# Time attention in half-key tiles: scores for the queries that see the keys, exchanged halves in the second tile, and layer-norm roots kept in PSUM

## The chip, the cores and the metric

The kernel runs on one core of a Trainium2 chip. The core has five engines with their own instruction streams: TensorE (PE, matrix products; PEld is its weight load), VectorE (DVE), ScalarE (ACT), GpSimd (POOL) and SyncE (SP, which issues transfers). Two memories matter: SBUF, the working memory with 128 partitions, and PSUM, eight banks of 512 fp32 elements a partition, into which TensorE writes. The metric is the device time of one execution in microseconds (us), the median of several runs. A profiled execution has its own time and a span, from its first to its last instruction.

## The reference: what is computed

One layer works on x of shape (2, 256, 128, 128): batch, time, band, channel, all fp32. Everything is 65,536 tokens of 128 channels.

```
xt = layernorm(x) by token, over time: for each band
x  = x + attention(xt, 4 heads of 32, key time <= query time)
xf = layernorm(x), over bands: for each time
x  = x + attention(xf, 4 heads of 32, |key band - query band| <= 16)
x  = x + W2 gelu(W1 layernorm(x) + b1) + b2
```

The change touches the first of the three, the attention over 256 times with its causal mask. A layer norm's root is 1/sqrt(variance + 1e-5) for each token.

## The kernel before

**Groups.** Work goes in groups of 512 tokens, four tiles of 128. There are 128 groups of time attention (`OverTime`), each with two bands (`s` = 0, 1) of 256 times, so that each band has a first tile of 128 keys and a second one. After them come 128 groups of attention over bands (`OverBands`) and 128 of the feed-forward (`FeedForward`), interleaved in runs of eight.

**Order.** `BoundedPath.run` (line 1046 on) is one loop over n, written out by hand: an iteration holds steps of several groups (n - 2 to n + 12), and each engine executes its instructions in exactly the order in which they stand there (`InOrder`, whose `pinned` is line 870: that is why every line of the profile reads L870, and why the tiles' names tell the operations apart). In the time stage an iteration n has, engine by engine:

- TensorE: the scores of two groups mixed (`time_scores`: second tiles of group n, first tiles of n + 1), then the row sums `rp` and the weighted values `op` of group n - 1 (`weigh`), the output product `yp` of n - 2, and the query, key and value products `qp`, `kp`, `vp` of n + 2.
- ScalarE: exponentials of heads 0 and 3 of the second tiles, of heads 1 and 2 of the first tiles, of heads 1 and 2 of the second tiles; `ln` and `r` (one over the row sums, by Ln and Exp) of n - 1; exponentials of heads 0 and 3 of the first tiles; then `qT` and `kT` out of PSUM, the root of group n + 5 (`root_by_scalar`: `lnv` by Ln, `root` by Exp with scale -1/2), and `v` out of PSUM.
- VectorE: statistics of group n + 5 (`stats`, `mv`), `normalize` (`xh`) and `turn` (`z`) of n + 4, the residual `res` of n - 2 (`finish`), three operations of `divide` for n - 1 (the last, `oT`, reads `op`), and the root of n + 5 made exact by one Newton step (`refine`: `vy`, `vy`, `rstd`, operations on 128x4 elements).
- GpSimd: the causal mask of the second tiles (`mask_second`), a sum of exponentials (`add`), the mask of the first tiles (`mask_first`), the other `add`, and the residual with its bias row (`bias`: `res<-x,orow`).
- SyncE: four transfers that write `turned` out of `z`, the fetch of `xnT`, the loads of x and the stores of the result.

**Scores.** For a head h, whose 32 channels lie on 32 partitions, `first_scores` multiplies 128 keys of the first tile with all 256 queries of the band, and `second_scores` 128 keys of the second tile with the 128 queries of the second tile. Each uses a 32-row strip of TensorE, so four heads can run side by side; their outputs lie in eight banks, one per head and tile. An fp32 product is two records of matmul in the trace.

**Banks.** The eight banks have roles that rotate from iteration to iteration. Banks a1 and a2 (first tiles of heads 1 and 2) always stay; they also take `yp` and `qp`. `rp` and `op` go to b0 and b3, which are the next iteration's a0 and b1:

```
b = self.banks
Attention.place = dict(rp=b["b0"], op=b["b3"], yp=b["a1"], qp=b["a2"], kp=b["b1"], vp=b["b2"])
...
self.banks = dict(
    a1=b["a1"], a2=b["a2"], b0=b["a0"], b3=b["a3"], a0=b["b0"], a3=b["b1"], b1=b["b3"], b2=b["b2"]
)
```

So the second-tile scores of head 1 overwrite the bank whose `op` was last read by `oT`, and wait for it.

Of the kernel before, what the change touches and what calls it, by code (L numbers as in the profile page):

```python
# [10 lines left out]
F32 = mybir.dt.float32  # L11
# [3 lines left out]
ALU = mybir.AluOpType  # L15
# [4 lines left out]
P = 128  # L20
H = 4
# [4 lines left out]
NT = 4  # L26
# [6 lines left out]
HALF = P // 2  # L33
# [47 lines left out]
def shifted_path(tc, k, x, out):  # L81
# [5 lines left out]
    with ExitStack() as ctx:  # L87
# [36 lines left out]
        def norm_transposed(src, w_col, b_col):  # L124
# [18 lines left out]
            return xnT  # L143

        def attention(src, dst, which, banks, mask, exp_after):


# [280 lines left out]
class Group:  # L428
# [30 lines left out]
        gpsimd.tensor_scalar(self.rstd, self.mv[:, :, 1], EPS, None, ALU.add)  # L459
        gpsimd.tensor_tensor(self.rstd, self.rstd, path.k.mhalf, ALU.pow)  # L460

    def root_by_scalar(self):

        path = self.path
        ln = path.small.tile([P, NT], F32, name="lnv")
        path.scalar.activation(ln, self.mv[:, :, 1], AF.Ln, bias=path.eps)
        self.root0 = path.small.tile([P, NT], F32, name="root0")
        path.scalar.activation(self.root0, ln, AF.Exp, scale=-0.5)

    def refine(self):  # L470

        path, vector, y = self.path, self.path.vector, self.root0
        t = path.small.tile([P, NT], F32, name="vy")
        vector.scalar_tensor_tensor(t, self.mv[:, :, 1], EPS, y, ALU.add, ALU.mult)
        vector.scalar_tensor_tensor(t, t, -0.5, y, ALU.mult, ALU.mult)
        self.rstd = path.small.tile([P, NT], F32, name="rstd", bufs=16)
        vector.scalar_tensor_tensor(self.rstd, t, 1.5, y, ALU.add, ALU.mult)
# [62 lines left out]
    def values(self):  # L540
        pass
# [19 lines left out]

class Attention(Group):
    which = None
    place = {}

    def bias(self):
# [23 lines left out]
    def values(self):  # L590
        path = self.path
        wv = path.k.wf[self.which][:, 2 * P : 3 * P]
        self.vp = path.bank([P, NT, P], "vp", self.place.get("vp"))
        for i in range(NT):
            product(path, self.vp[:, i], self.xnT[:, i * P : (i + 1) * P], wv)

    def take_values(self):
        path = self.path
# [43 lines left out]
def rows_of(h):  # L642
    return slice(h * D, (h + 1) * D)


def product(path, out, weights, x, start=True, stop=True):


    for c in range(P // D):
        path.tensor.matmul(out[rows_of(c)], weights[:, rows_of(c)], x, start=start, stop=stop)  # L650


class OverTime(Attention):

    which = 0
    early, late = (1, 2), (0, 3)

    def first_tiles(self):  # L660
# [10 lines left out]

    def first_scores(self, h, s):
        r, a = rows_of(h), 2 * s * P
        self.path.tensor.matmul(
            self.s0[h][:, s], self.kT[r, a : a + P], self.qT[r, a : a + 2 * P], start=True, stop=True
        )

    def second_scores(self, h, s):
        r, a = rows_of(h), (2 * s + 1) * P
        self.path.tensor.matmul(  # L680
            self.s1[h][:, s], self.kT[r, a : a + P], self.qT[r, a : a + P], start=True, stop=True
        )

    def first_weights(self, heads):
        for h in heads:
# [3 lines left out]
        for h in heads:  # L689
            self.path.scalar.activation(self.p1[:, :, h, 0], self.s1[h], AF.Exp)  # L690

    def mask(self, blk):
        path = self.path
        path.gpsimd.affine_select(
            out=blk, in_=blk, compare_op=ALU.is_ge, fill=path.zero, base=0,
            pattern=[[0, 2], [0, H], [1, P]], channel_multiplier=-1,
        )

    def mask_first(self):
        self.mask(self.p0[:, :, :, 0:P])  # L700

    def mask_second(self):
        self.mask(self.p1[:, :, :, 0])

    def add(self, s):
        self.path.gpsimd.tensor_tensor(self.p1[:, s, :, 1], self.p1[:, s, :, 0], self.p0[:, s, :, P : 2 * P], ALU.add)
# [168 lines left out]
class BoundedPath:  # L875
# [170 lines left out]
    def run(self, x, out):  # L1046
        groups = list(self.groups(x, out))

        def do(n, *names):
            if 0 <= n < len(groups):  # L1050
                for name in names:
                    getattr(groups[n], name)()

        def at(n, kind):
            return 0 <= n < len(groups) and isinstance(groups[n], kind)

        def do_at(n, kind, *names):
            if at(n, kind):
                do(n, *names)


        run0 = [i for i in range(len(groups)) if at(i, OverBands)][: RUN // NT]
        due = dict(zip(run0, (-5, -4, -4, -3, -1, 0, 1, 2)))
        due = {n: [i for i in run0 if run0[0] + due[i] == n] for n in range(-12, len(groups) + 2)}
        A = RUN // NT

        self.scalar.preload_act_table_set(EXP_SET)
        for n in range(-12, len(groups) + 2):
            feeds = [at(n - 2 + i, FeedForward) for i in range(5)]
            bands = [at(n - 2 + i, OverBands) for i in range(5)]  # L1070
            turn = feeds[2] and bands[1]
            old, new = (groups[i] if at(i, OverTime) else None for i in (n, n + 1))
            if bands[2] and feeds[1]:
                self.scalar.preload_act_table_set(EXP_SET)
            do_at(n + 4, FeedForward, "root")
            do(n, "first_half", "first_function", "first_mask")
            if old is not None or new is not None:
                time_scores(old, new)
                b = self.banks
                Attention.place = dict(rp=b["b0"], op=b["b3"], yp=b["a1"], qp=b["a2"], kp=b["b1"], vp=b["b2"])  # L1080
            else:
                Attention.place = {}
            if old is not None:
                old.second_weights(old.late)
            if new is not None:
                new.first_weights(new.early)
            if old is not None:
                old.second_weights(old.early)
                old.mask_second()
                old.add(0)  # L1090
            if turn:
                do(n, "second_half", "second_function")
            do_at(n + 3, OverTime, "fetch")
            do_at(n + 2, (OverBands, FeedForward), "fetch")

            for i in (2 * n + 12, 2 * n + 13) if n < -2 else (n + 10,) if n < 2 else ():
                if i >= NT:
                    do(i, "load")
            if n < -8 or n >= 0:
                do(n + 12, "load")  # L1100
            if n >= 0:
                do_at(n + 5, OverTime, "statistics")
                for i in due[n]:
                    do(i, "statistics")
            do_at(n + 3, (OverBands, FeedForward), "normalize", "turn")
            do_at(n + 4, OverTime, "normalize", "turn")
            if n < 0:
                do(n + 5, "statistics")
            do_at(n + 5, FeedForward, "statistics")
            if n == -4:  # L1110
                self.fold_rest()
                self.warm()
            do(n - 1, "weigh")
            do(n - 1, "invert_exactly" if turn else "invert")
            if new is not None:
                new.first_weights(new.late)
                new.mask_first()
            if old is not None:
                old.add(1)
            if bands[2] or turn or old is not None:  # L1120
                do(n - 2, "output", "finish")
            do(n - 1, "divide")
            if not turn:
                do(n, "second_half", "second_function")
            if n in run0:
                do(n, "bias")
            if not bands[2] and old is None:
                do_at(n, FeedForward, "bias")
                do_at(n + A, OverBands, "bias")
                if at(n - 1, FeedForward) and at(n - 2, OverBands):  # L1130
                    do_at(n + A - 1, OverBands, "statistics", "root")
                if not turn:
                    do_at(n + A, OverBands, "statistics", "root")
            do_at(n + 2, OverTime, "queries_keys", "take_query", "take_key")
            do_at(n + 1, OverBands, "queries_keys", "take_query", "take_key")
            do_at(n + 5, OverTime, "root_by_scalar", "refine")
            for i in due[n]:
                do(i, "root_by_scalar", "refine")
            do_at(n, OverTime, "bias")
            if not bands[2] and not turn and old is None:  # L1140
                do(n - 2, "output", "finish")
            do_at(n + 2, OverTime, "values", "take_values")
            do_at(n + 1, OverBands, "values", "take_values")
            if old is not None or new is not None:
# [5 lines that stand above are left out]
# [69 lines left out]
```

## Time and profile before

| what | us |
|---|---|
| median of 3 runs | 2706.51 (2705.36 to 2706.72) |
| profiled execution: its time | 2703.05 |
| profiled execution: its span | 2701.3 |
| TensorE busy | 2662.7 |
| VectorE busy | 2280.2 |
| ScalarE busy | 1848.3 |
| GpSimd busy | 1868.7 |
| time stage, from one group's scores to the next | 7.311 (mean over groups 8 to 124) |

The time stage takes the first 950 us or so of the span; its first scores start at 30.7 us and its last ones near 950. A line of groups reads: line, engine, operation, output<-inputs, shapes, count, then busy us in total and mean ns of one, then idle time before them. A line of the timeline reads: start in us, length in us, engine, line, operation, output<-inputs, shape, and how many in a row are merged. TensorE's ends are modelled, and busy TensorE is not TensorE at its peak; starts are the better guide.

### The profile page before, as it was taken

The page shows a single profiled execution, that of the slowest core. Times are in us where ns is not written, and L with a number is a line of the kernel's source. Part 1 is how long each engine was busy: PE and PEld are TensorE (multiplying, and loading weights), DVE is VectorE, ACT ScalarE, POOL GpSimd, SP SyncE. Part 2 cuts the span into 40 slices and gives each one's busy share as a digit, 9 for nine tenths or more (in the row PEclk, how much of TensorE's full clock was granted, in tenths as well). Part 3 has the DMA queues.
Part 4 walks back from the last instruction along what each step waited for, and adds up shares of the span by engine and source line. Part 5 has one row for each costly group of instructions (what it writes and reads, how often), then busy time and mean ns, then how long its engine had stood idle before and what let it go on. Part 6 is the DMA issues. An engine that isn't in the chain of part 4 may idle for free.

```text
span 2701.3 us, 148062 instructions
## 1 busy us (share of the span) xinstructions
PE 2662.7 (99%) x64566; PEld 1824.9 (68%) x64566; DVE 2280.2 (84%) x6708; ACT 1848.3 (68%) x3620; POOL 1868.7 (69%) x2169
## 2 busy tenths in 40 slices
PE   7999999999999999999999999999999999999998
PEld 5667666767676666666666666666666766666665
DVE  7999999999999997868769779688697796886874
ACT  6888888888888874655746646557456465565573
POOL 3888788878888886667657666666676666665762
PEclk9999999999999999999999999999999999999999
DMA  5555555555555535445444444454444444544433
GB/s 151 142 151 143 145 151 144 149 146 142 151 144 148 150 101 129 111 121 132 109 127 124 115 125 116 121 128 116 120 124 117 121 119 121 135 108 121 129 100 82
DMA packets 471477, 346.55 MB, mean 128 GB/s; under 512 B 43296, under 2 KB 405152, under 8 KB 470816
## 3 DMA queue, kind: packets, MB, share of 16 engines
q1 hardware_dynamic: 469568, 335.92, 47.8%
q8 instruction: 508, 8.32, 1.3%
q14 instruction: 153, 1.25, 0.2%
q10 hardware_dynamic: 1248, 1.05, 0.2%
HBM read 169.03 MB, written 167.77 MB: 125 GB/s over the span
## 4 chain that ended last, share of the span: by engine, by line
PE 83%; DVE 13%; DMA 2%; issue 1%; ACT 0%; SPq 0%; DVEq 0%; ACTq 0%
PE bank L870 83%; DVE xh L870 3%; DVE bank L870 3%; DVE stats L870 2%; DVE z L870 2%; DVE u L870 2%; DMA xnT<-turned 1%; DVE x L870 1%; DVE mv L870 1%; DMA turned<-z 0%; SPq L870 0%; DMA x<-in_x 0%; DVE oT L870 0%; DMA rows_sb<-in_rows 0%; ACT p L870 0%
## 5 line engine op out<-in xcount | busy, mean ns | idle before, releaser
L870 ACT ACTIVATE hT<-bank,b 128x512 f32<-128x512 f32 x512 | 347.1, 688 | 536.0 <-PE bank L870 517.0
L870 POOL TENSOR_SCALAR_AFFINE_SELECT pf<-pf 128x512 f32<-128x512 f32 x768 | 478.5, 638 | 246.8 <-ACT pf L870 220.5
L870 DVE TENSOR_SCALAR xh<-x,mv,rstd 128x160 f32<-128x160 f32 x1536 | 597.1, 431 | 14.2
L870 PEld LDWEIGHTS bank<-w2T_sb,hT 128*32 128x32 f32 x16384 | 459.7, 110 | 63.1 <-issue 38.8
L870 PE MATMUL bank<-xnT,wf 128*32 128x512 f32 x4096 | 488.6, 592 | 2.0 <-ACT p L870 2.0
L870 PE MATMUL bank<-w2T_sb,hT 128*32 128x128 f32 x16384 | 477.5, 273 | 0.5 <-ACT hT L870 0.2
L870 PE MATMUL bank<-xnT,w1f 128*32 128x512 f32 x4096 | 474.2, 592 | 0.0
L870 ACT ACTIVATE p<-bank 128x512 f32<-128x512 f32 (+1 forms) x1024 | 417.3, 499 | 15.1 <-PE bank L870 3.8
L870 POOL TENSOR_SCALAR_AFFINE_SELECT p<-p 128x1024 f32<-128x1024 f32 x256 | 280.9, 1097 | 188.2 <-ACT p L870 188.2
L870 DVE TENSOR_TENSOR res<-bank,res 128x512 f32<-128x512 f32 x256 | 171.1, 668 | 229.1 <-PE bank L870 227.2
L870 PE MATMUL bank<-qT,kT 32*64 32x80 f32 (+2 forms) x12288 | 346.9, 275 | 4.2 <-DVE oT L870 2.2
L870 PEld LDWEIGHTS bank<-wf,xnT 128*32 128x32 f32 x8192 | 235.5, 110 | 154.4 <-issue 135.9
L870 PEld LDWEIGHTS bank<-qT,kT 32*64 32x64 f32 (+1 forms) x12288 | 298.0, 148 | 58.7 <-ACT kT L870 48.2
L870 POOL TENSOR_TENSOR p<-p,p 128x512 f32<-128x512 f32 x256 | 329.2, 1286 | 10.7
L870 DVE BATCH_NORM_STATS2 stats<-x 128x6 f32<-128x128 f32 x1536 | 326.9, 275 | 0.9 <-DMA x<-in_x 0.9
L870 ACT ACTIVATE pf<-bank 128x512 f32<-128x512 f32 x512 | 267.1, 602 | 50.9 <-PE bank L870 48.8
L870 DVE STREAM_TRANSPOSE z<-xh 128x512 f32<-128x512 f32 x384 | 273.3, 712 | 13.4
L870 PEld LDWEIGHTS bank<-xnT,w1f 128*32 128x32 f32 x4096 | 156.4, 110 | 189.4 <-issue 159.3
L870 POOL TENSOR_SCALAR rstd<-mv 128x4 f32<-128x4 f32 x248 | 56.7, 229 | 312.8 <-DVE mv L870 311.3
L870 PE MATMUL bank<-wf,xnT 128*32 128x128 f32 x8192 | 272.6, 273 | 0.0
L870 PE MATMUL bank<-wn,oT 128*32 128x128 f32 x8192 | 271.7, 273 | 0.0
L870 POOL TENSOR_TENSOR rstd<-rstd,mhalf 128x4 f32<-128x4 f32 x248 | 257.0, 1036 | 20.7
(93 smaller groups left out, 3770.3 us busy)
## 6 DMA issues: line engine op xcount, KB each, us to landing
turned<-z SPq DMA_DIRECT2D x1536, 64.0 KB, 2.2
xnT<-turned SPq DMA_DIRECT2D x384, 256.0 KB, 3.1
x<-in_x SPq DMA_DIRECT2D x128, 256.0 KB, 4.1
x<-res SPq DMA_DIRECT2D x256, 128.0 KB, 2.4
x<-x SPq DMA_DIRECT2D x128, 256.0 KB, 4.2
out<-res SPq DMA_DIRECT2D x256, 128.0 KB, 2.5
w1T_sb<-in_w1T ACTq DMA_DIRECT2D x1, 256.0 KB, 6.5
w2T_sb<-in_w2T ACTq DMA_DIRECT2D x1, 256.0 KB, 7.9
```

Of the source, the lines that this page charges most:

```text
L870: return self.tc.keep_in_program_order(emit(*args, **kwargs))
```

## The change

Four things change in the time attention, and nothing in the other two parts.

1. A first-tile score product is cut into two, of 64 keys each: keys 0 to 63 with all 256 queries, keys 64 to 127 with the 192 queries from 64 on, which are those that can see them. Positions that are left out keep what the bank held, and the mask sets them to zero after the exponential.
2. A second-tile score product is cut likewise: keys 64 to 127 with the queries 64 to 127, keys 0 to 63 with all 128. Their halves are exchanged: keys 64 to 127 go to partitions 0 to 63, keys 0 to 63 to partitions 64 to 127. So that the weights meet the right values, the value products of the second tiles (1 and 3) put their rows in the same exchanged order (`turn=2`). The mask of the second tile becomes two selects, one for each half of the partitions.
3. The root by ScalarE is written to bank a2 in PSUM, four columns of it, in the place where the first-tile exponentials of head 2 have just been read from. It is made right after the exponentials of heads 1 and 2 of the first tiles, in the iteration after the one where it stood.
4. The exact root (`refine`) moves from the end of the iteration, behind `divide`, to just ahead of `normalize` of the same group.

The instructions that each engine executes in a steady iteration are otherwise the same and in the same order.

```diff
-    def root_by_scalar(self):
+    def root_by_scalar(self, to=None):
...
-        self.root0 = path.small.tile([P, NT], F32, name="root0")
+        self.root0 = path.small.tile([P, NT], F32, name="root0") if to is None else to
         path.scalar.activation(self.root0, ln, AF.Exp, scale=-0.5)
+
+    def root_in_bank(self):
+        path = self.path
+        self.root_by_scalar(path.ps[path.banks["a2"]][:, 0:NT])
...
-            product(path, self.vp[:, i], self.xnT[:, i * P : (i + 1) * P], wv)
+            product(path, self.vp[:, i], self.xnT[:, i * P : (i + 1) * P], wv, turn=2 if i in self.swapped else 0)
...
-        path.tensor.matmul(out[rows_of(c)], weights[:, rows_of(c)], x, start=start, stop=stop)
+        path.tensor.matmul(out[rows_of(c)], weights[:, rows_of((c + turn) % NT)], x, start=start, stop=stop)
...
     which = 0
+    swapped = (1, 3)
...
     def first_scores(self, h, s):
         r, a = rows_of(h), 2 * s * P
-        self.path.tensor.matmul(
-            self.s0[h][:, s], self.kT[r, a : a + P], self.qT[r, a : a + 2 * P], start=True, stop=True
-        )
+        for e in range(0, P, HALF):
+            self.path.tensor.matmul(
+                self.s0[h][e : e + HALF, s, e:], self.kT[r, a + e : a + e + HALF], self.qT[r, a + e : a + 2 * P],
+                start=True, stop=True,
+            )
 
     def second_scores(self, h, s):
         r, a = rows_of(h), (2 * s + 1) * P
-        self.path.tensor.matmul(
-            self.s1[h][:, s], self.kT[r, a : a + P], self.qT[r, a : a + P], start=True, stop=True
-        )
+        for e in range(0, P, HALF):
+            q = P - HALF - e
+            self.path.tensor.matmul(
+                self.s1[h][e : e + HALF, s, q:], self.kT[r, a + q : a + q + HALF], self.qT[r, a + q : a + P],
+                start=True, stop=True,
+            )
...
     def mask_second(self):
-        self.mask(self.p1[:, :, :, 0])
+        self.mask(self.p1[0:HALF, :, :, 0], -HALF)
+        self.mask(self.p1[HALF:P, :, :, 0, 0:HALF])
...
             if new is not None:
                 new.first_weights(new.early)
+            do_at(n + 4, OverTime, "root_in_bank")
             if old is not None:
                 old.second_weights(old.early)
...
-            do_at(n + 4, OverTime, "normalize", "turn")
+            do_at(n + 4, OverTime, "refine", "normalize", "turn")
...
-            do_at(n + 5, OverTime, "root_by_scalar", "refine")
```

More of the change, by code (lines that the diff above doesn't have):

```diff
@@ L563 @@
     which = None
+    swapped = ()
     place = {}
@@ L643, in rows_of, with product @@
     return slice(h * D, (h + 1) * D)
-def product(path, out, weights, x, start=True, stop=True):
+def product(path, out, weights, x, start=True, stop=True, turn=0):
     for c in range(P // D):
-        path.tensor.matmul(out[rows_of(c)], weights[:, rows_of(c)], x, start=start, stop=stop)
+        path.tensor.matmul(out[rows_of(c)], weights[:, rows_of((c + turn) % NT)], x, start=start, stop=stop)
 class OverTime(Attention):
     which = 0
+    swapped = (1, 3)
     early, late = (1, 2), (0, 3)
@@ L690, in second_weights, with mask @@
             self.path.scalar.activation(self.p1[:, :, h, 0], self.s1[h], AF.Exp)
-    def mask(self, blk):
+    def mask(self, blk, base=0):
         path = self.path
         path.gpsimd.affine_select(
-            out=blk, in_=blk, compare_op=ALU.is_ge, fill=path.zero, base=0,
-            pattern=[[0, 2], [0, H], [1, P]], channel_multiplier=-1,
+            out=blk, in_=blk, compare_op=ALU.is_ge, fill=path.zero, base=base,
+            pattern=[[0, 2], [0, H], [1, blk.shape[-1]]], channel_multiplier=-1,
         )
```

## The prediction

> **What bounds the kernel now.** I read the page first: the span, the busy line and the 40 slices. TensorE is busy in every slice; VectorE is at 90% or more in the first thirteen full slices, which are the time attention that the change edits, and falls off after them.
>
> ```profile
> span 2701.3 us, 148062 instructions
> ...
> PE 2662.7 (99%) x64566; PEld 1824.9 (68%) x64566; DVE 2280.2 (84%) x6708; ACT 1848.3 (68%) x3620; POOL 1868.7 (69%) x2169
> ...
> DVE  7999999999999997868769779688697796886874
> ```
>
> "PE 99%" does not tell which of the two sets the pace, so I went to the timeline of one group (start, length, engine, operation), then to the groups by form of the whole stage.
>
> ```profile
> 502.28 0.30 ACT L870 ACTIVATE lnv<-mv,eps 128x4 f32<-128x4 f32 x1
> ...
> 502.53 1.63 PE L870 MATMUL bank<-qT,kT 32*128 32x128 f32 x32
> 502.61 0.20 ACT L870 ACTIVATE root<-lnv 128x4 f32<-128x4 f32 x1
> ...
> 503.08 1.26 POOL L870 TENSOR_TENSOR res<-x,orow 128x512 f32<-128x512 f32 x1
> ...
> 503.31 1.05 DVE L870 SCALAR_TENSOR_TENSOR vy<-mv,root 128x4 f32<-128x4 f32 x1
> 503.38 2.19 ACT L870 ACTIVATE p<-bank 128x256 f32<-128x256 f32 x6
> ...
> 504.09 1.07 PE L870 MATMUL bank<-p,ones 128*32 128x256 f32 x16
> 504.40 0.17 DVE L870 SCALAR_TENSOR_TENSOR vy<-vy,root 128x4 f32<-128x4 f32 x1
> 504.60 0.16 DVE L870 SCALAR_TENSOR_TENSOR rstd<-vy,root 128x4 f32<-128x4 f32 x1
> 504.68 0.86 DVE L870 BATCH_NORM_STATS2 stats<-x 128x6 f32<-128x128 f32 x4
> ...
> 505.74 1.58 DVE L870 TENSOR_SCALAR xh<-x,mv,rstd 128x160 f32<-128x160 f32 x4
> ...
> 509.86 1.62 PE L870 MATMUL bank<-qT,kT 32*128 32x128 f32 x32
> ...
> 510.02 0.69 DVE L870 TENSOR_TENSOR oT<-bank,u 128x512 f32<-128x512 f32 x1
> ```
>
> ```profile
> L870 DVE SCALAR_TENSOR_TENSOR vy<-mv,root 128x4 f32<-128x4 f32 x114 | 120.1, 1053 | 0.0
> ...
> L870 DVE SCALAR_TENSOR_TENSOR vy<-vy,root 128x4 f32<-128x4 f32 x114 | 18.6, 163 | 3.9
> ```
>
> Call the first weight load of a score step S (502.53). The next is at 509.86; over groups 8 to 124 the mean period is 7.311 us, and about 124 periods make the stage. VectorE's starts follow each other without a hole over 100 ns all the way round: it is the bound. Its strangest entry is vy, 1053 ns for four elements, where the same operation a line later takes 163: vy ends at 504.37, just after POOL's res (503.08 + 1.26 = 504.34). TensorE is nearly level: its weight load for the last four second-tile scores (heads 1 and 2) starts at 503.448, 52 ns after oT ends (503.396), because head 1's bank is the one whose op oT still reads. That wait cost about 0.05 us.
>
> **What the Trainium skill says.** "SBUF — State Buffer", section "Who interferes with whom": a VectorE instruction with two SBUF inputs contends with a GpSimd instruction that reads SBUF, one with a single SBUF input does not. The trace agrees: vy (both in SBUF) stretches to 1053 ns, while u and oT (one input in PSUM) stay at 692 beside running POOL work. "TensorEngine Tiling (Array Packing)", section "Key Properties": tiles run independently and changing the mode drains the array; the trace shows four streams side by side in the score step and about 0.09 us between stages of different tiling. "TensorE: Matmul & The Clock Gate", section "Architectural detail: the array is 16× 32×32, not 1× 128×128": VectorE and ScalarE are strict first-in first-out. So a VectorE wait holds all that stands behind it, which decides below.
>
> **Part by part, per group.**
>
> *Scores.* One row strip (a head) streams 2 x (256 + 128) = 768 columns today. At 213 ns a record of 256 columns and two records a matmul that is 1.28 us; with the first load (0.107), the 0.05 wait and the 0.09 drain it makes the 1.56 from 502.53 to 504.09. Afterwards each half strip streams 2 x (256 + 64) or 2 x (192 + 128), 640 either way: 1.07 us, with a load of 0.053. Left alone the step would be 1.07 + 0.05 + 0.09 and some skew, about 1.27. The records double to 64; the band scores already run such a step in 1.00 us (1422.32 to 1423.32), their last 24 records at 21 ns each, so issue stays below streaming. TensorE alone would need 7.31 - 0.29 = 7.02. Exchanging the halves and turning two value products adds no instruction. Exponentials keep their sizes; where no query sees a key they run over what the bank held, and the mask clears it.
>
> *Second mask.* One select of 1024 elements a partition (1.10) becomes one of 1024 and one of 512, each on 64 partitions. The nearest rows give 1.10 and 0.64; if half the partitions cost half, 0.55 and 0.32; if the smaller cost like the larger, 2.19. I take 1.74 less overlap, +0.58 on POOL, hidden in its 1.30 idle before the select.
>
> *Refinement.* vy reads the root from PSUM: 1053 becomes about 165 (0.15 to 0.25; no row shows this form). VectorE's work drops to about 6.5.
>
> *Order.* The two root activations no longer stand before the v copy; they follow the first-tile exponentials of heads 1 and 2, and the three refinements now stand after the statistics and **ahead of xh**. So xh, z, res, three divisions and oT wait for a root made in the same group; in the old order the root was half a microsecond old when wanted. The transpose's four DMA issues and the fetch on SP come with it, about 0.3 later in the group; xnT is used over a period after landing, no cost. The projection of queries waits for the refinement's end (S + 3.4) and starts near S + 4.6: no cost.
>
> **The new chain, from S.** Head 0's second scores end 0.05 earlier (smaller load), so the first exponential starts at 0.80 instead of 0.85. The starts of the next operations follow by 0.281, 0.264, 0.478 and 0.477 (measured starts of the exponentials), Ln to Exp 0.331, Exp 0.206: the root is there at 2.84. Handing over 0.035, three refinements 3 x 0.197 = 0.591: xh at 3.46. From xh's start to oT's end today: 510.714 - 505.744 = 4.97, unchanged. oT ends at 8.43. The last scores of the *next* group wait for it: 0.052 handover, 0.053 load, four records of 128 columns 0.436, drain 0.09, together 0.63: the row sums start at 9.06. From row sums to the following S: 509.86 - 504.091 = 5.77. That is S two groups later: 14.83, a period of **7.415**. The other floors are lower: TensorE 7.02, VectorE 6.5, ACT about 6.4, and POOL's chain (second select at 3.5, its five operations end at 8.9, then row sums' second half to S, 5.53: 14.4 over two groups, 7.22). So VectorE idles about 0.75 us a group, oT ends 1.02 after the next S where TensorE would like it by 0.75, and the score step measures about 1.65 instead of 1.56: both savings are there and the wait eats them. 124 x (7.415 - 7.311) = +12.9 us; fill and drain of the stage I take as nothing (a few one-off steps, +-2). Against the profiled 2703.05 (span 2701.3) that gives 2716; the median of the runs is 3.5 higher, so 2706.5 + 13 = 2719.5.
>
> **Rivals.** (1) *The freed VectorE is enough*: if the two-group chain is 0.22 us shorter than I sum, the period falls to 7.31, and below that it gains. The chain has four hand-overs that I read off other places. For it: VectorE loses 0.89 of work and TensorE 0.29. Against: even a root 0.2 earlier only breaks even. With POOL's chain next the period is 7.22, -11 us, 2695; with both loose 7.02, 2670. This ends on the other side; its place is xh's wait for the root, its price 0.75 us of VectorE idling. (2) *Even*: the chain within 0.1 of 14.62. (3) *POOL takes over*: selects at 2.19 make its chain 14.9, period 7.45, 2724; with TensorE also waiting for the sums, up to 7.55, 2736. For it: POOL has 0.3 us of slack before the row sums' second half. (4) *The edit doesn't do what it says*: root in PSUM does not release vy. Then vy runs on to the end of POOL's res, but res would end near S + 10.1, 2.7 after the next S, before vy starts: hardly any cost in the new order.
>
> **How the numbers follow.** The measurement tells about 0.2% (5.4 us) from nothing. Chain as summed, slower: 0.58; POOL on top, slower: 0.10; even: 0.14; rival 1, faster: 0.18. The chain's sum is uncertain by about 0.2 in 14.83, 0.1 a period, 12 us: its own range is 2708 to 2733. To leave out no more than two in ten the range reaches into rival 1 at POOL's floor and to POOL's slower bound: 2695 to 2737.
>
> **What would show it.** The first vy back at about 165 ns, preceded by VectorE idling some 0.75 us that ends on ACT's root; oT ending near S + 1.0 of the next group and TensorE's last scores loading right after it; score step about 1.65; POOL's selects 1.10 and about 0.6; period 7.4. Wrong if VectorE shows no wait for the root, if the weight load of the last scores doesn't follow oT, or if the score step shrinks to 1.3: then rival 1 holds, and the gain is that of TensorE.

## The result and the profile after

The changed kernel takes 2731.64 us (median of 4 runs, 2728.96 to 2732.01) beside 2706.61 for the kernel before: a ratio of 1.0091, with a 95% interval of 1.0074 to 1.0109. It is slower, by 25.0 us; 13 were forecast. The number lies inside the forecast range.

I read the profile in the order used before. The page first: span, busy line, and the VectorE row of the 40 slices.

```profile
span 2729.8 us, 156632 instructions
...
PE 2688.3 (98%) x68662; PEld 1831.7 (67%) x68662; DVE 2191.9 (80%) x6708; ACT 1858.7 (68%) x3620; POOL 1953.7 (72%) x2297
...
DVE  5888888888888898769779688687696786886974
```

VectorE lost 88 us of work (2280.2 to 2191.9), and in the time stage its slices went from 9 down to 8: it has holes now. The 4096 added TensorE records are the cut scores (128 groups x 32). The timeline of one group shows the holes.

```profile
511.52 1.45 PEld L882 LDWEIGHTS bank<-qT,kT 32*64 32x64 f32 x64 [0.20 <-ACT kT L882]
511.52 1.69 PE L882 MATMUL bank<-qT,kT 32*64 32x64 f32 x64
...
511.80 0.69 DVE L882 TENSOR_TENSOR oT<-bank,u 128x512 f32<-128x512 f32 x1
512.39 1.64 ACT L882 ACTIVATE p<-bank 128x256 f32<-128x256 f32 x4
...
513.14 1.07 PE L882 MATMUL bank<-p,ones 128*32 128x256 f32 x16
...
513.89 0.32 ACT L882 ACTIVATE lnv<-mv,eps 128x4 f32<-128x4 f32 x1
...
514.24 0.18 ACT L882 ACTIVATE bank<-lnv 128x4 f32<-128x4 f32 x1
...
514.45 0.16 DVE L882 SCALAR_TENSOR_TENSOR vy<-mv,bank 128x4 f32<-128x4 f32 x1 [0.90 <-ACT bank L882]
...
515.03 1.61 DVE L882 TENSOR_SCALAR xh<-x,mv,rstd 128x160 f32<-128x160 f32 x4
515.07 1.82 POOL L882 TENSOR_SCALAR_AFFINE_SELECT p<-p 64x1024 f32<-64x1024 f32 x2 [0.81 <-ACT p L882]
...
518.91 1.34 PE L882 MATMUL bank<-qT,kT 32*64 32x64 f32 x46
...
519.34 0.69 DVE L882 TENSOR_TENSOR oT<-bank,u 128x512 f32<-128x512 f32 x1
```

S is 511.52 here. The root (`bank<-lnv`) ends at 514.42, VectorE starts vy 30 ns later and had stood idle for 0.90 us. xh follows at 515.03, and the chain behind it ends with oT at 519.34 + 0.69 = 520.03, which is 1.12 us after the next S (518.91). The scores that wait for oT's bank come after that: in every one of the groups 8 to 121 a weight load of the score step starts 0.05 us after oT ends, with a spread of 1 ns (the 23rd of 32 loads before, the 49th of 64 now). In the mean oT ends at S + 1.05, where it ended at S + 0.85 before. By form, over the stage from 45 to 940 us, the first refinement reads:

```profile
L882 DVE SCALAR_TENSOR_TENSOR vy<-mv,bank 128x4 f32<-128x4 f32 x120 | 19.0, 159 | 102.2 <-ACT bank L882 102.2
```

159 ns where it was 1053, and 102.2 us of waiting for the root in 120 groups, 0.85 each: the 0.89 that the short vy gives back is spent just ahead of it.

**Where the 25 us are.** From here on, "period" is the mean from one S to the next over groups 8 to 121, and "step" is the mean from S to the first load of the row sums. The period went from 7.311 to 7.463 us and the step from 1.547 to 1.700; what lies between the row sums and the next S is 5.764 in both kernels. 124 x 0.152 = 18.8 us. The last score step of the stage begins 25.6 us later than before (974.1 beside 948.5), so some 6.5 us more were lost outside the steady part. (The two profiled spans differ by 28.5 us, 25.6 of them by this point; the medians differ by 25.0.) Most of it is in the first groups:

```profile
26.03 0.18 ACT L882 ACTIVATE bank<-lnv 128x4 f32<-128x4 f32 x1 [5.80 <-PE bank L882]
26.23 0.16 DVE L882 SCALAR_TENSOR_TENSOR vy<-mv,bank 128x4 f32<-128x4 f32 x1 [5.28 <-ACT bank L882]
...
35.97 3.64 PE L882 MATMUL bank<-xnT,wf 128*32 128x512 f32 x16 [2.97 <-DVE rstd L882]
```

The second root waits 5.80 us for a bank that TensorE's warm-up products (`bank<-wf,ones`) have written. The second query projection comes 2.97 us after TensorE's last work: its weight load waits for an exponential that stands behind the root on ScalarE, its products for the refinement, which ends 0.06 later. It then takes 3.64 us, where the first one took 1.92. In the kernel before, the second projection had waited 1.15 us, for an exponential, and began at 32.97; the fourth score step begins at 55.7 us instead of 48.0.

### The profile page after: what moved, and what is told of

Its sections match the earlier page's. It is cut to its first block, busy times and chain, and to the rows that moved or that the text cites. A ratio compares the mean times of both kernels' runs of the same rounds, so it can differ in the third digit from the quotient of the medians.

```text
span 2729.8 us, 156632 instructions
## 1 busy us (share of the span) xinstructions
PE 2688.3 (98%) x68662; PEld 1831.7 (67%) x68662; DVE 2191.9 (80%) x6708; ACT 1858.7 (68%) x3620; POOL 1953.7 (72%) x2297
## 3 DMA queue, kind: packets, MB, share of 16 engines
q10 hardware_dynamic: 1248, 1.05, 0.2%
## 4 chain that ended last, share of the span: by engine, by line
PE 83%; DVE 13%; DMA 2%; issue 1%; ACT 0%; SPq 0%; DVEq 0%; ACTq 0%
PE bank L882 83%; DVE xh L882 3%; DVE bank L882 3%; DVE stats L882 2%; DVE z L882 2%; DVE u L882 2%; DMA xnT<-turned 1%; DVE x L882 1%; DVE mv L882 1%; DMA turned<-z 1%; SPq L882 0%; DVE oT L882 0%; ACT p L882 0%; DMA f_wiT_sb<-in_f_wiT 0%; DVE res L882 0%
## 5 line engine op out<-in xcount | busy, mean ns | idle before, releaser
L882 DVE TENSOR_SCALAR xh<-x,mv,rstd 128x160 f32<-128x160 f32 x1536 | 600.9, 433 | 18.8
L882 POOL TENSOR_SCALAR_AFFINE_SELECT p<-p 128x1024 f32<-128x1024 f32 (+2 forms) x384 | 364.9, 950 | 130.1 <-ACT p L882 121.8
L882 ACT ACTIVATE p<-bank 128x512 f32<-128x512 f32 (+1 forms) x1024 | 428.2, 487 | 22.4 <-DVE mv L882 2.5
L882 PE MATMUL bank<-qT,kT 32*64 32x80 f32 (+4 forms) x16384 | 366.1, 276 | 5.2 <-DVE oT L882 2.6
L882 PEld LDWEIGHTS bank<-qT,kT 32*64 32x64 f32 x16384 | 302.5, 130 | 68.0 <-ACT kT L882 49.2
```

The lines of the kernel that those rows point to most:

```text
L882: return self.tc.keep_in_program_order(emit(*args, **kwargs))
```

## The experiments

My theory after the result: nearly the whole loss is the place of the root (made and used in the same group, in the order of the change), with a part in the stage's first groups; the cut scores are harmless. The rival: the cut scores themselves, with 64 products and GpSimd's longer mask, hold the stage, and the wait for the root is only where it shows. All ratios are to the kernel before on the same chip, with 95% intervals.

### e1_scores_only: cut scores, root as before

```diff
-            do_at(n + 4, OverTime, "root_in_bank")
...
-            do_at(n + 4, OverTime, "refine", "normalize", "turn")
+            do_at(n + 4, OverTime, "normalize", "turn")
...
+            do_at(n + 5, OverTime, "root_by_scalar", "refine")
```

> Only the scores, their exchanged halves and the second mask are changed; roots and their exact step stay as they were before. Theory (chain through the root): the whole loss of the changed kernel comes from the root's place, so this run lacks it, but it meets another wait: POOL's sequence is about 0.7 us longer, vy still has both inputs in SBUF and waits for POOL, now for two of its operations in turn, so the period goes from 7.31 to about 7.6 and the time to about 2745 us (2715 to 2750). Rival A (cutting the scores costs TensorE by itself, in 64 records): about 2730, with vy at 1053 ns as before. Rival B (the freed TensorE is all that counts): 2675 to 2700.

Measured: 2726.56 us, ratio 1.0081 (1.0064 to 1.0098); period 7.483, step 1.720. The cut alone, with the root in its old place, costs about as much as the whole change. The time lies in the range that I gave, but nearer to rival A's 2730 than to my 2745; what decides is the timeline of a group:

```profile
508.46 1.87 PE L882 MATMUL bank<-qT,kT 32*64 32x64 f32 x64
508.54 0.21 ACT L882 ACTIVATE root<-lnv 128x4 f32<-128x4 f32 x1
508.92 0.69 DVE L882 TENSOR_TENSOR oT<-bank,u 128x512 f32<-128x512 f32 x1
509.52 0.18 DVE L882 SCALAR_TENSOR_TENSOR vy<-mv,root 128x4 f32<-128x4 f32 x1
509.64 1.28 POOL L882 TENSOR_TENSOR res<-x,orow 128x512 f32<-128x512 f32 x1
509.74 1.20 DVE L882 SCALAR_TENSOR_TENSOR vy<-vy,root 128x4 f32<-128x4 f32 x1
```

The longer mask moves GpSimd's res later. The first vy slips through ahead of it in 0.18, and the *second* one, with both inputs in SBUF too, starts 0.10 after res and ends at 510.94, 0.02 after res ends (510.92). The stretched operation is the same loss at another place, and it now ends at S + 2.48; in the kernel before it ended at S + 1.84 (504.37 - 502.53). The three refinements take 1.57 us a group over the stage (384 + 1005 + 180 ns), where they took 1.38 (1053 + 163 + 160); VectorE has no idle time before them, and the 0.19 more is nearly what the period grew by (0.172). As in the changed kernel, a load of the score step starts 0.05 us after oT's end in every group. So the cut gains nothing with the roots and the order as they were.

### e2_root_only: the root's move, uncut scores

```diff
-    swapped = (1, 3)
...
-        for e in range(0, P, HALF):
-            self.path.tensor.matmul(
-                self.s0[h][e : e + HALF, s, e:], self.kT[r, a + e : a + e + HALF], self.qT[r, a + e : a + 2 * P],
-                start=True, stop=True,
-            )
+        self.path.tensor.matmul(
+            self.s0[h][:, s], self.kT[r, a : a + P], self.qT[r, a : a + 2 * P], start=True, stop=True
+        )
```

(and the second-tile scores, the mask and the value products likewise as before)

> Only the root is changed (PSUM bank, after the first exponentials, exact step ahead of normalize); scores and masks as before. Theory: the two-group chain is as long as in the changed kernel, 14.93 us, plus 0.05 for the larger last weight load: period about 7.48, and the fill of the stage costs the same 6.5 us, so about 2734 us, vy at 160 ns with VectorE idle 0.7 to 0.9 us before it. Rival A: no loss, 2707 or a little below.

Measured: 2731.24 us, ratio 1.0098 (1.0082 to 1.0115); period 7.475, step 1.712; vy takes 158 ns after 102.1 us of waiting for ScalarE's root in 120 groups. Parts 3 and 4 of the change alone lose what the change loses; the cut takes 0.012 us off this period. So each half of the change, alone, costs what both cost together: the losses are alternatives, not a sum, because each is a way of making oT later for the next group's scores (S + 1.07 in e1_scores_only, S + 1.01 here, S + 1.05 in the changed kernel, S + 0.85 before).

### e3_root_ahead: cut scores, root a group ahead

```diff
-            do_at(n + 4, OverTime, "root_in_bank")
+            if n >= 0:
+                do_at(n + 5, OverTime, "statistics", "root_in_bank")
...
-                do_at(n + 5, OverTime, "statistics")
...
-            do_at(n + 4, OverTime, "refine", "normalize", "turn")
+            do_at(n + 4, OverTime, "normalize")
+            if n >= 0:
+                do_at(n + 5, OverTime, "refine")
+            do_at(n + 4, OverTime, "turn")
...
+            if n < 0:
+                do_at(n + 5, OverTime, "root_by_scalar", "refine")
```

The root stays in the bank, but it is that of the next group, whose statistics move ahead with it; VectorE refines it after xh, so that xh finds its own ready. The first groups keep the old order.

> The changed kernel, but the root is made one group ahead: statistics of group n + 5 stand before its root in the same iteration, the exact step stands between xh and z of group n + 4, and nothing in that iteration needs it. In the fill (n below 0) the roots stay as before the change. Theory: the chain through the root is gone, oT is early, no wait for it in the last scores; the period is then TensorE's own, 7.03 if its score step shrinks to 1.27 as forecast, 7.34 if it stays at the 1.58 that the changed kernel's third score step shows, or POOL's chain, 7.22: 2672 to 2710 us, at least 20 us below the changed kernel. Rival A (the cut scores are what costs): stays above 2725.

Measured: 2713.22 us, ratio 1.0033 (1.0021 to 1.0046); period 7.352, step 1.587: between my range, which ended at 2710, and the rival's. The timeline:

```profile
505.50 0.69 DVE L882 TENSOR_TENSOR oT<-bank,u 128x512 f32<-128x512 f32 x1
...
505.83 1.66 PE L882 MATMUL bank<-qT,kT 32*64 32x64 f32 x64
507.17 1.58 DVE L882 TENSOR_SCALAR xh<-x,mv,rstd 128x160 f32<-128x160 f32 x4
...
508.55 0.18 ACT L882 ACTIVATE bank<-lnv 128x4 f32<-128x4 f32 x1
508.75 0.16 DVE L882 SCALAR_TENSOR_TENSOR vy<-mv,bank 128x4 f32<-128x4 f32 x1
...
510.80 0.69 DVE L882 TENSOR_TENSOR res<-bank,res 128x512 f32<-128x512 f32 x1 [0.77 <-PE bank L882]
```

The wait for the root is gone, and oT is out at 506.19, S + 0.36 here (S + 0.37 in the mean). VectorE's idle time stands before res now, and it is TensorE for which it waits (90.1 us in 118 groups): VectorE isn't the bound any more. The place of the root was 0.111 us of the period (7.463 - 7.352). But the period is still above the one before, and the step, 1.587 instead of my 1.27, is all that differs: 1.587 + 5.764 = 7.351. Neither theory stands whole. The wait for the root was most of the loss; behind it the cut scores are slow by themselves. (With the same scores, e1_scores_only stands at 1.720: 0.133 of its step is the wait for oT.)

### e4_root_ahead_old_scores: the same without the cut

The order of e3_root_ahead with the uncut scores, mask and value products of e2_root_only.

> As the run with the root one group ahead, but with the scores and masks of before. Theory: VectorE falls to about 6.5 us a group and TensorE alone is left: 7.31 less its 0.05 wait, 7.26, so 2698 to 2707 us. The difference to the run with the cut scores is what the cut scores are worth on TensorE: up to 28 us if the step shrinks by 0.29, nothing if it doesn't shrink.

Measured: 2703.59 us, ratio 0.9994 (0.9985 to 1.0002); period 7.287, step 1.522. With the wait out of the way and the score products in the order in which they stand, the cut makes the step longer by 0.065 us (1.587 against 1.522), although each half strip streams 640 columns instead of 768. The order alone gains 0.024 a group, 3 us over 124; the runs can't tell this from nothing.

### e5_ahead_sbuf: does it take PSUM?

```diff
-                do_at(n + 5, OverTime, "statistics", "root_in_bank")
+                do_at(n + 5, OverTime, "statistics", "root_by_scalar")
```

(against e3_root_ahead: the root goes to its SBUF tile)

> As the run with the root one group ahead and the cut scores (2713 us), but the root is written to SBUF as before the change. vy then has both inputs in SBUF, and starts 2.93 us after the scores, where POOL's res has just ended. If the PSUM root is worth only what it saves of POOL's lock, this run is within 5 us of 2713, vy at 160 ns in most groups and longer in those where res is still running; if the lock bites in every group, vy is at 500 ns or more, but VectorE has 0.7 us to spare, so still below 2720.

Measured: 2712.51 us, ratio 1.0024 (1.0016 to 1.0033), period 7.352 as with the bank. vy takes 169 ns in the mean, with both inputs in SBUF: at this place of the order GpSimd is not in the middle of a long instruction. In this order the place alone frees vy, and the bank isn't needed; whether the bank alone would free it too is seen in e10_need_root_later, below.

### e6_old_fill: the changed kernel with the first groups' roots as before

```diff
-            do_at(n + 4, OverTime, "root_in_bank")
+            if n >= 0:
+                do_at(n + 4, OverTime, "root_in_bank")
...
-            do_at(n + 4, OverTime, "refine", "normalize", "turn")
+            if n >= 0:
+                do_at(n + 4, OverTime, "refine")
+            do_at(n + 4, OverTime, "normalize", "turn")
...
+            if n < -1:
+                do_at(n + 5, OverTime, "root_by_scalar", "refine")
```

> The changed kernel, with the roots of the first four groups made as before the change (SBUF, at the end of the iteration), so that in the fill of the stage no root shares bank a2 with the warm-up and query products. Theory: the fill gives back most of the 7 us between the first steps of the two traces (third to fourth score step at 55.7 against 48.0), the period stays 7.46: 2724 to 2728 us against 2731. Rival: the loss lies all in the period, 2731 as the changed kernel.

Measured: 2725.72 us, ratio 1.0075 (1.0058 to 1.0091), period 7.461. That is 5.9 us less than the changed kernel by the medians, 4 by the ratios, at the same period, and the fourth score step begins at 49.6 us instead of 55.7. This is the part of the loss that isn't in the steady state, and it is due to the roots of the first groups. The edit moves them to SBUF and to their old place at once, so it doesn't tell which of the two costs. Nor is the figure sharp: in e4 and e11, whose code differs in the order of the score products alone, the fourth step begins at 52.3 and 48.8.

### e7_ahead_order and e8_ahead_all_queries: count of products, or columns?

Both are e3_root_ahead with one thing changed. e7_ahead_order draws the second band's first-tile scores of heads 1 and 2 ahead of those of heads 0 and 3. e8_ahead_all_queries lets all 64-key products run over all queries, so that 64 records stream the 768 columns of old.

```diff
-        (0, 1, 0), (1, 0, 0), (2, 0, 0), (3, 1, 0), (0, 1, 1), (3, 1, 1), (0, 0, 0), (3, 0, 0),
-        (1, 0, 1), (2, 0, 1), (0, 0, 1), (3, 0, 1), (1, 1, 0), (2, 1, 0), (1, 1, 1), (2, 1, 1),
+        (0, 1, 0), (1, 0, 0), (2, 0, 0), (3, 1, 0), (0, 1, 1), (3, 1, 1), (1, 0, 1), (2, 0, 1),
+        (0, 0, 0), (3, 0, 0), (0, 0, 1), (3, 0, 1), (1, 1, 0), (2, 1, 0), (1, 1, 1), (2, 1, 1),
```

> As the run with the root one group ahead and the cut scores (2713 us, score step 1.587), but in the score step the second band's first-tile scores of heads 1 and 2 stand before those of heads 0 and 3 (places 7 and 8 instead of 9 and 10 of 16). Theory now: the step is not held by streaming (1.07) but by how far ahead TensorE takes its 128 instructions in order, head 2's second products coming late; with them earlier the step falls to 1.40 to 1.50 and the time to 2690 to 2703. Rival: the tail after the copy of v holds it, then the step stays at 1.58 and the time at 2713.

```diff
-                self.s0[h][e : e + HALF, s, e:], self.kT[r, a + e : a + e + HALF], self.qT[r, a + e : a + 2 * P],
+                self.s0[h][e : e + HALF, s], self.kT[r, a + e : a + e + HALF], self.qT[r, a : a + 2 * P],
...
-                self.s1[h][e : e + HALF, s, q:], self.kT[r, a + q : a + q + HALF], self.qT[r, a + q : a + P],
+                self.s1[h][e : e + HALF, s], self.kT[r, a + q : a + q + HALF], self.qT[r, a : a + P],
```

> As the run with the root one group ahead and the cut scores, but each product of 64 keys takes all 256 or 128 queries, so that a half strip streams 768 columns again (1.28 us) in the same 128 instructions. If the number and order of instructions hold the step, it stays within 0.06 of 1.587 and the time within 8 us of 2713; if streaming holds it, the step grows by about 0.21 to 1.80 and the time to about 2738.

| kernel | records, columns of a half strip | step | us | ratio (95%) |
|---|---|---|---|---|
| e4_root_ahead_old_scores | 32, 768 | 1.522 | 2703.59 | 0.9994 (0.9985 to 1.0002) |
| e8_ahead_all_queries | 64, 768 | 1.696 | 2724.34 | 1.0070 (1.0054 to 1.0087) |
| e3_root_ahead | 64, 640 | 1.587 | 2713.22 | 1.0033 (1.0021 to 1.0046) |
| e7_ahead_order | 64, 640, other order | 1.537 | 2706.29 | 1.0004 (0.9995 to 1.0013) |

The first two rows stream the same columns: twice the records cost 0.174 us. The next one saves 128 of 768 columns, which at 213 ns a record of 256 columns and two records a product is 0.21, and gets 0.109 for it. So leaving out columns is worth something, less than it should be, and cutting the instructions costs more than that. e7 and e8 both fell between the two values expected of them: neither streaming alone nor count alone sets the step.

The weight loads of one score step of e3_root_ahead, in three stretches (from:to, length, busy time and number of the loads in it; then TensorE's clock, DMA share and GB/s), show one place where the 64 products stall:

```profile
505.82:506.37 0.55, 0.55 (x38) 1.00 0.55 134
506.37:506.50 0.13, 0.12 (x6) 1.00 0.77 197
506.50:507.20 0.70, 0.69 (x26) 1.00 0.70 160
```

38 + 26 are all 64 loads; the 6 in the middle are still running from the first stretch, and none *starts* there. The 38th load is at S + 0.537 and the 39th at S + 0.687 in the mean of 114 groups, and the 39th spreads by less than a nanosecond. After the pause the next three come 16 to 17 ns apart. In e7, with another order, the 38th is at 0.522 and the 39th again at 0.687; in e8 the pause is there too. The uncut step has only 32 loads and never gets so far. "Tiles operate independently" in the words of the Trainium skill ("TensorEngine Tiling (Array Packing)", section "Key Properties"); the pause is one of all tiles at once, at the same time after S in three orders, so I suspect what feeds them. That is not shown, nor is what comes late, nor how much of the 0.174 the pause makes.

### e9_ahead_by_need, e10_need_root_later, e11_uncut_order: can the cut be made to pay?

e9_ahead_by_need is e3_root_ahead with the half products as entries of their own, in the order in which their banks and key halves come free:

```diff
-    for h, second, s in (
+    for h, second, s, e in (
+        (0, 1, 0, 0), (0, 1, 0, 1), (1, 0, 0, 0), (1, 0, 0, 1), (2, 0, 0, 0), (2, 0, 0, 1), (3, 1, 0, 0), (3, 1, 0, 1),
+        (0, 1, 1, 0), (3, 1, 1, 0), (0, 1, 1, 1), (3, 1, 1, 1), (0, 0, 0, 0), (3, 0, 0, 0), (1, 0, 1, 1), (2, 0, 1, 1),
+        (0, 0, 0, 1), (3, 0, 0, 1), (1, 0, 1, 0), (2, 0, 1, 0), (0, 0, 1, 0), (3, 0, 1, 0), (1, 1, 0, 1), (2, 1, 0, 1),
+        (0, 0, 1, 1), (3, 0, 1, 1), (1, 1, 0, 0), (2, 1, 0, 0), (1, 1, 1, 1), (2, 1, 1, 1), (1, 1, 1, 0), (2, 1, 1, 0),
```

> Cut scores, the root one group ahead as in e3_root_ahead, and in the score step alone the 32 half products are put in the order in which their banks and key halves come free. If the score step of e3 (1.587 us) is long because products stand behind others that still wait for a bank, it falls to 1.34 to 1.45. Then TensorE could do a group in about 7.1, but GpSimd's chain (mask from S + 3.55, its sums ended at S + 9.0, and 5.52 from there to the next S but one: 14.57 for two groups) holds the period at 7.28: 2700 to 2705. If it is long because TensorE does not get its 64 products fast enough (the pause after the 38th weight load, until S + 0.687), the step stays at 1.54 or more with the pause in the same place: 2706 to 2713.

e10_need_root_later moves the root behind the second-tile exponentials of heads 1 and 2:

```diff
             if n >= 0:
-                do_at(n + 5, OverTime, "statistics", "root_in_bank")
...
+                if n >= 0:
+                    do_at(n + 5, OverTime, "statistics", "root_in_bank")
```

(the second place is behind `old.second_weights(old.early)`)

> As e9_ahead_by_need, and ScalarE makes the root after the second-tile exponentials of heads 1 and 2 instead of before them, so that GpSimd's second mask starts some 0.45 us earlier (S + 3.1). If GpSimd's chain was what held e9_ahead_by_need, its two-group chain is 14.1 and the period 7.06 to 7.2: 2676 to 2695, faster than both kernels. If the supply of products holds the step at 1.54 or more, the earlier mask gains nothing and it stays at 2704 to 2713.

e11_uncut_order is e4_root_ahead_old_scores, the uncut one, with the order of products of e7_ahead_order (its diff above).

> As e4_root_ahead_old_scores (uncut scores, masks and value products of the kernel before, root one group ahead), with the score products in the order of e7_ahead_order. It tells whether the gain of e9_ahead_by_need (period 7.253, step 1.489) is that of the cut or of the order. If of the order, the uncut step, 1.522 with the old order, falls to its streaming, 1.28 + 0.107 + 0.09 = 1.48, and the period to 7.25: 2697 to 2700. If of the cut, the uncut step stays at 1.51 to 1.54, because its last loads follow the bank that oT reads and not the order: 2702 to 2706.

| kernel | period | step | us | ratio (95%) |
|---|---|---|---|---|
| e9_ahead_by_need | 7.253 | 1.489 | 2698.32 | 0.9976 (0.9966 to 0.9986) |
| e10_need_root_later | 7.255 | 1.491 | 2700.57 | 0.9981 (0.9972 to 0.9990) |
| e11_uncut_order | 7.287 | 1.523 | 2703.71 | 0.9992 (0.9983 to 1.0000) |

e9 is faster than both kernels, by 7.6 us against the one before. Its step fell by 0.098 against e3, with the pause in the same place (38th load at S + 0.538, 39th at S + 0.688), and it is not down to 1.34, which the first theory wanted. Both expectations of e9 were half right, and neither has the cause: the last weight load of the step is no earlier than in e3 (S + 1.288 and 1.284), so products that stood behind others were not what it cured. What shrank is the time from that load to the row sums, from 0.303 us to 0.201, in every group within a nanosecond. e3's order ends on a piece with 128 queries, e9's on one with 64, and the last loads follow each other by 0.109 in e3 and 0.058 in e9. e7 gained in the other way: its last load is at 1.235, and 0.303 follow.

e10 missed: it starts the mask 0.41 us earlier (S + 3.15 instead of 3.56) and gains nothing. So GpSimd's chain did not hold e9, although I had summed it to 7.28; TensorE did. The waits of its products in the stage, from 45 to 940 us of e9, are one line:

```profile
PE bank L884 <- POOL p L884: 0.2, 1, 0.2
```

and from the row sums to the next S it takes the 5.764 of every other kernel. So 1.489 + 5.764 is the period. (The 5.764 are not all products: in every kernel the step's first weight load waits 0.20 us for ScalarE's copy of kT.)

e11 shows whose gain e9 has, and it falls on the side of the cut: the uncut step doesn't answer to e7's order (1.522, 1.523; last load at 1.206 in both), and as every uncut second-tile product takes 128 queries, no order lets it end on 64. Other orders of the uncut products were not tried. The cut with a fitting order is worth 0.034 us a group over the uncut kernel with the same root, 4.2 us; the root a group ahead is worth 0.024, 3.0 us. Together 7.2 of the 7.6 measured.

## Why the prediction was right, and where not

**Direction and mechanism: right.** "xh, z, res, three divisions and oT wait for a root made in the same group": shown by the trace (0.85 us of idling ahead of vy, 0.75 forecast) and by e3, which takes that wait away and with it 0.111 of the period.

**The chain, term by term** (mean of groups 8 to 121, us after S):

| step | forecast | measured |
|---|---|---|
| first exponential | 0.80 | 0.872 |
| root ready | 2.84 | 2.900 |
| vy | about 0.165 | 0.159 |
| xh | 3.46 | 3.513 |
| oT ends | 8.43 | 8.513 |
| row sums of the next group, from oT's end | 0.63 | 0.651 |
| from there to S | 5.77 | 5.764 |
| two periods | 14.83 | 14.928 |

Each link is within 0.1, and the largest miss is the first: "Head 0's second scores end 0.05 earlier (smaller load)". The exponential that reads them starts 0.02 later than before. The load is smaller, but the cut products' results were not out earlier; what delays them inside the step was not tested apart. By xh the miss is 0.05; that, with 0.03 from xh to oT and 0.02 behind oT, makes the 0.10 in two periods, 0.05 a period, 6 us of the 12 that were missing.

**The fill: mis-sized.** "fill and drain of the stage I take as nothing": it was some 6.5 us by the traces and 4 to 6 by e6_old_fill. I had followed the root's new bank and place in the steady order, and not in the first groups, where the same bank holds warm-up products and the query projection. These 6 us and the 6 above make about the difference of 12 between 13 forecast and 25 measured.

**The step that fell: TensorE's floor.** "Left alone the step would be 1.07 + 0.05 + 0.09 and some skew, about 1.27", "issue stays below streaming", "TensorE alone would need 7.31 - 0.29 = 7.02". Left alone in e3 it was 1.587, a floor of 7.35, above the kernel before. I had read from the band scores that 64 records are no load on the issue. They are: at equal streaming the doubled count costs 0.174. The step that I read it from says so too. Its 64 loads serve eight half strips with 80 columns a record; at the 213 ns for 256 columns that is an estimate of 0.53 us of streaming, and the step took 1.00. No load starts there between the 33rd and the 34th, from 0.26 to 0.33 us, and the last 24 start 13 ns apart, not 21. The sum for the uncut step was loose as well: its four terms give 1.53, not 1.56, and the wait for oT, put at 0.05, was worth 0.025 (1.547 before, 1.522 in e4). It was luck that this did no harm to the forecast: the chain through the root was longer still, by 0.11; but rival 1's "with both loose 7.02, 2670" was never there to be had in this order, and the best of these kernels stands at 7.253. Nor was VectorE alone the bound of the kernel before: with its 0.89 us taken off and no new wait, e4 gains 0.024 a group, since TensorE stood just behind it.

**The other parts.** GpSimd's two selects took 1.090 and 0.661, 1.75 together, as forecast (1.74): a select over half the partitions takes as long as one over all (1.099). It still idled 0.79 us a group ahead of the mask, so rival 3 didn't come. Rival 1 needed a two-group chain 0.22 shorter than summed; it was 0.10 longer. Rival 4 can't be judged in the changed kernel: vy is at 159 ns, but GpSimd is idle when it runs (from 514.26, where res ends, to 515.07 in the group shown). e10_need_root_later judges it, for there vy and its two followers start in the middle of a select:

```profile
509.70 1.81 POOL L884 TENSOR_SCALAR_AFFINE_SELECT p<-p 64x1024 f32<-64x1024 f32 x2 [0.54 <-ACT p L884]
510.04 0.16 DVE L884 SCALAR_TENSOR_TENSOR vy<-mv,bank 128x4 f32<-128x4 f32 x1 [0.57 <-ACT bank L884]
```

All 369 such operations of that run, with the root in the bank, take 157 to 160 ns. In e5_ahead_sbuf, with the root in SBUF, seven meet the same select, and take 999 to 1091. So the root in PSUM does free vy, as forecast, and rival 4 is out. And "VectorE loses 0.89" needs the other half of what e1 shows: the stretch belongs not to that vy but to whichever small operation with two SBUF inputs meets a running GpSimd instruction.

## What to carry to other kernels

Freeing an engine of a stretched operation gains nothing if the same edit puts a wait for a younger value at that place: look first at how old each operand is when it is wanted, and take it from one group ahead (here 11 us, by the ratios of e6 and e3, for a few lines of order). Two edits that each free a different engine can each be eaten by the same hand-over, so undo them one at a time and don't add up their effects. Before cutting products to save columns, measure a step with the doubled count and the old columns: the count had a price of 0.174 us here, beside a saving of 0.21 on paper, and only an order that ends on the smallest pieces left something over. And where a value gets a new home in a rotating resource, follow the first few groups as well as the steady ones: here they were about a quarter of the loss.

## What was not expected of the hardware

- In a score step of 64 products on eight half strips, no weight load starts between the 38th (S + 0.52 to 0.54) and S + 0.687, whatever the order of products (e3, e7, e9) or their columns (e8). What holds them is open.
- The order of instructions changed the length of a step of cut products by 0.098 us (1.587 to 1.489), all of it after the last weight load: 0.303 us from there to the row sums where the last piece takes 128 queries (e3, e7, e8), 0.201 where it takes 64 (e9, e10). The one other order of the uncut products that was tried changed nothing (1.522 to 1.523).
- A 128x4 VectorE operation with two SBUF inputs that starts 0.10 us after a GpSimd addition lasts to 0.02 after its end (1.20 us instead of 0.16), and one that starts 0.12 ahead of the addition takes 0.18. With the root in PSUM it takes 0.16 beside running GpSimd work (e10). That is the contention which the Trainium skill tells of ("SBUF — State Buffer", section "Who interferes with whom"); its size for so small an operation, all of the rest of GpSimd's instruction, is what these traces add.
